# Own rows of a message step kept as three bfloat16 parts and spread by a one-hot matrix, in a sparse two-layer graph kernel

## The chip, the core and the metric

The kernel runs on one core of a Trainium2 chip. A core has a matrix engine (TensorE, in the profile PE, with its weight loads listed apart as PEld), a vector engine (VectorE, DVE), a scalar engine (ScalarE, ACT), a general engine (GpSimd, POOL) that here issues the gathers, and a queue for plain transfers (SyncE, SP). The metric is the device time of one execution in microseconds. Three timed runs of the kernel before gave 449.30, 445.47 and 449.06 us, so the median is 449.06 us. One more execution was recorded by the hardware profiler; it took 498.16 us, with a span of 496.4 us from its first to its last instruction.

## What is computed

Two graph layers over 2708 nodes with 128 features and a sparse 0/1 adjacency matrix. Layer 0 is attention with four heads over the neighbours of each node, gated, added to x and normalised. Layer 1, which the change is about, is a message layer; with everything that does not matter here left out, the reference is

```python
s = node_feats @ msg_w[:, :D].T
d = node_feats @ msg_w[:, D:].T
messages = gelu(s[:, None, :] + d[None, :, :] + msg_b)
aggregated = einsum('ijd,ij->id', messages, adj)
new_feats = concatenate([node_feats, aggregated], -1) @ upd_w.T + upd_b
h = gelu(new_feats) + node_feats
...
return (h - mu) / sqrt(var + LN_EPS) * ln_w + ln_b
```

followed by adding x and one more normalisation. So every edge (i, j) needs the row d[j] of its neighbour, the row s[i] + msg_b of its own node, and the sum of the two.

## The kernel before

The nodes are cut into 22 blocks of at most R = 126 rows, the blocks into nine groups: block 0 alone, six groups of three, one of two, and the last block alone. Each block's edges are listed in chunks of 128; there are 103 chunks. In layer 0 the adjacency rows of a block are loaded, its edges found and numbered, the neighbours' rows fetched by indirect transfers (POOL, L1116), and the attention sums made. `finish` closes a group: gate, normalisation, the new x in `xs`, its transpose in `xT`. Then `half(b, 1, ...)` makes d for each block of the group (PE L1274, ACT copy L1276 into the right half of `sd`) and sends it to the table `d_t` in DRAM. When all of `d_t` is written, layer 1 begins.

Layer 1 runs over 33 jobs of up to four chunks, the last group of blocks first and block 0 last; function `message` builds one:

- POOL fetches d of the neighbours, one indirect transfer for each chunk (L1318), into a buffer `g`, of which there are six.
- At a block's first job, `half(b, 0, ...)` makes s of the block in the left half of `sd` (PE L1274, ACT L1276). Row R of `sd` holds msg_b.
- `spreader` turns the one-hot staircase `E16` (bfloat16, row r is one from the first edge of row r on) into edge-to-row indicators: a bfloat16 matmul with the difference matrix `diff` (PE L1128) and an ACT copy into the float32 buffer `t32` (L1131).
- PE multiplies `t32` with s (L1335, float32, one product for each chunk), so that each edge gets its own row's s + msg_b in a bank of the pool `pq`.
- DVE adds g and that bank (L1339), ACT takes the gelu (L1342), and PE adds the messages up by rows with an indicator `s32` that DVE makes from the row numbers (L1327, PE L1353), into a bank of `pk`.

After a group's last job `update` follows: L1371 (ACT), L1375 and L1376 (PE), L1379 (ACT), L1385 (PE), then some thirty small DVE operations from L1388 on, and the output (SP, L1406).

Accumulator memory has eight banks: `pk` 2, `pm` 2, `pq` 3, `pr` 1. Every engine works through its instructions strictly in the order in which the program issues them. That order is worked out when the kernel is built, by the class `Board`: each operation is given a cost, the ones it comes after, a rank, and a lag, which is the time from its end to the moment when another engine can use it (`LAG`: 0.35 us for PE, 0.25 for DVE, 0.3 for ACT). The board simulates the engines with these figures and issues the operations in the order of their simulated starts. The true waits on the chip follow from the data, not from the board.

## Time and profile before

| | value |
|---|---|
| timed runs, median of three | 449.06 us |
| profiled execution, its own time | 498.16 us |
| its span | 496.4 us |
| mean granted TensorE clock in it | 0.748 |
| first gather of layer 1 (L1318) issued | 305.12 us |
| last gather of layer 1 done issuing | 468.25 us |
| gathers of layer 1 | 103, mean 957 ns |

Read the page like this: the busy shares of engines are averages over two layers with different limits, so each layer has to be read by itself. A "releaser" is what ended an engine's idle time; "remote" or "another core or an unknown queue" is put there when no recorded instruction or transfer fits. The profiled execution is 49.1 us longer than the median of the timed runs.

### The profile page before, as it was taken

How to read it: one execution, taken by the hardware profiler on the slowest of the kernel's cores; microseconds unless marked ns; L12 is line 12 of the kernel's file. 1: busy time of each engine (PE TensorE's matmuls, PEld its weight loads, DVE VectorE, ACT ScalarE, POOL GpSimd, SP SyncE). 2: the span in 40 equal slices, each digit the busy share in tenths (PEclk: the TensorE clock that was granted, in tenths of full speed). 3: DMA queues.
4: the chain of work that ended last, by engine and by line, in shares of the span. 5: the costliest groups of instructions: out<-in, count | busy, mean ns of one | idle time of the engine just before them, and what ended most of it. 6: DMA issues, size and time to landing. Idle time of an engine off the chain costs nothing.

```text
span 496.4 us, 5950 instructions
## 1 busy us (share of the span) xinstructions
PE 302.9 (61%) x1474; PEld 237.7 (48%) x1474; DVE 317.3 (64%) x1461; ACT 253.7 (51%) x587; POOL 224.2 (45%) x313
## 2 busy tenths in 40 slices
PE   3657786867785866649666356406484767274750
PEld 2334464745464645436556235405363656253650
DVE  4859787768676869848873775105457685463363
ACT  2366677647565858848766378205352233131310
POOL 7300467565533525262535103773664555566400
PEclk9769769688877878977695656555977797788765
DMA  7955949897899695851779988824421122122100
GB/s 180 237 139 191 282 111 262 226 267 239 291 245 245 190 234 128 258 156 33 217 241 231 251 239 264 200 54 131 114 53 44 43 60 51 34 61 65 33 15 11
DMA packets 31488, 78.51 MB, mean 158 GB/s; under 512 B 5776, under 2 KB 17131, under 8 KB 31439
## 3 DMA queue, kind: packets, MB, share of 16 engines
q1 hardware_dynamic: 21830, 55.06, 38.1%
q0 software_dynamic: 9520, 22.91, 18.8%
q8 instruction: 13, 0.21, 0.2%
q14 instruction: 30, 0.25, 0.2%
q10 hardware_dynamic: 95, 0.09, 0.1%
HBM read 72.38 MB, written 5.66 MB: 157 GB/s over the span
## 4 chain that ended last, share of the span: by engine, by line
PE 25%; DVE 23%; DMA 18%; issue 11%; another core or an unknown queue 8%; POOL 7%; ACT 6%; SPq 0%; DVEq 0%; POOLq 0%
DMA g<-kv_t,idx 12%; POOL g L1116 5%; PE pq L1335 4%; PE pk L1353 4%; ACT junk L993 2%; PE pk L954 2%; PE pm L866 2%; DMA kv_t<-kv 2%; DVE raw L959 2%; PE pm L1128 2%; PE pq L1087 2%; PE pr L1166 2%; POOL g L1318 2%; DMA sd<-in_x_dram 2%
## 5 line engine op out<-in xcount | busy, mean ns | idle before, releaser
L1116 POOL DMA_INDIRECT g<-kv_t,idx x103 | 99.8, 969 | 137.5 <-DMA abuf<-in_adj_dram 30.6
L1318 POOL DMA_INDIRECT g<-d_t,idx x103 | 98.5, 957 | 93.9 <-issue 55.2
L999 ACT ACTIVATE junk<-abuf,minus_one 126x1356 bf16<-126x1356 f32 (+15 forms) x44 | 62.8, 1427 | 7.9 <-DMA abuf<-in_adj_dram 7.9
L1131 ACT COPY t<-pm 127x384 f32<-127x384 f32 (+3 forms) x75 | 33.0, 453 | 66.1 <-remote 37.3
L1087 PE MATMUL pq<-rq,t 127*128 127x146 f32 (+3 forms) x206 | 49.8, 390 | 24.5 <-DVE qe L1147 14.5
L993 ACT ACTIVATE junk<-abuf 126x1356 bf16<-126x1356 uint32 (+15 forms) x44 | 58.8, 1335 | 0.2
L1335 PE MATMUL pq<-sd,t 127*128 127x128 f32 x206 | 37.7, 335 | 33.4 <-DVE kv L1339 15.2
L1087 PEld LDWEIGHTS pq<-rq,t 127*128 127x128 f32 x206 | 41.1, 255 | 32.2 <-DVE qe L1147 18.2
L1166 PE MATMUL pr<-val,s 128*126 128x136 f32 x206 | 47.2, 379 | 14.2 <-DVE val L1156 10.7
L1327 DVE TENSOR_TENSOR s<-iota,rid 128x504 f32<-128x504 f32 (+3 forms) x33 | 18.2, 565 | 58.0 <-remote 39.6
L1335 PEld LDWEIGHTS pq<-sd,t 127*128 127x128 f32 x206 | 34.8, 246 | 38.4 <-issue 29.4
L1166 PEld LDWEIGHTS pr<-val,s 128*126 128x126 f32 x206 | 39.9, 267 | 21.1 <-DVE val L1156 10.4
L954 PE MATMUL pk<-abuf,lkey 128*128 128x452 bf16 (+2 forms) x134 | 41.2, 411 | 11.8 <-DMA abuf<-in_adj_dram 4.2
L1353 PE MATMUL pk<-s,kv 128*128 128x126 f32 (+4 forms) x206 | 37.5, 334 | 5.5 <-ACT kv L1342 4.6
L1353 PEld LDWEIGHTS pk<-s,kv 128*128 128x128 f32 x206 | 34.0, 242 | 9.7 <-ACT kv L1342 7.4
L1147 DVE TENSOR_TENSOR qe<-pq,g 128x384 f32<-128x384 f32 (+2 forms) x42 | 20.1, 479 | 27.5 <-DMA g<-kv_t,idx 23.7
L1128 PE MATMUL pm<-E,diff 127*127 127x384 bf16 (+3 forms) x75 | 27.1, 377 | 16.0 <-ACT t L1131 4.4
L1274 PE MATMUL pm<-fwT,fxT 128*126 128x128 f32 x88 | 22.7, 365 | 14.8 <-issue 6.1
L959 DVE MAX8 raw<-pk 128x8 f32<-128x452 f32 (+39 forms) x59 | 24.9, 456 | 8.6 <-PE pk L954 3.8
L1274 PEld LDWEIGHTS pm<-fwT,fxT 128*126 128x126 f32 x88 | 18.8, 262 | 22.5 <-issue 10.1
L1342 ACT ACTIVATE kv<-kv 128x512 f32<-128x512 f32 (+3 forms) x33 | 17.3, 535 | 23.7 <-DVE kv L1339 15.8
L1339 DVE TENSOR_TENSOR kv<-g,pq 128x512 f32<-128x512 f32 (+3 forms) x33 | 18.3, 566 | 13.3 <-DMA g<-d_t,idx 12.7
(188 smaller groups left out, 628.0 us busy)
## 6 DMA issues: line engine op xcount, KB each, us to landing
abuf<-in_adj_dram SPq DMA_DIRECT2D x35, 667.4 KB
abuf<-in_adj_dram SPq DMA_DIRECT2D x35, 665.4 KB
kv_t<-kv SPq DMA_DIRECT2D x5, 528.0 KB
g<-kv_t,idx POOLq DMA_INDIRECT x103
g<-d_t,idx POOLq DMA_INDIRECT x103
xs<-in_x_dram POOLq DMA_DIRECT2D x22, 63.0 KB
sd<-in_x_dram SPq DMA_DIRECT2D x3, 448.0 KB
d_t<-sd SPq DMA_DIRECT2D x14, 63.0 KB
```

The lines of the kernel that those rows point to most:

```text
L954: nc.tensor.matmul(pt["at"][:, : c1 - c0], lkeys[k], low[:, 2 * c0 + 1 : 2 * c1 : 2], start=k == 0, stop=k == fold - 1)
L959: nc.vector.max(keyed["at"][:, k * CAP : (k + 1) * CAP], pt["at"][:, s0 - lo : s1 - lo])
L993: return board.add("ACT", 0.4 + 0.00085 * w, lambda: nc.scalar.activation(one.tile([P, FOLD * KW], BF16, name="junk")[:rows, :w], at.bitca ...
L999: return board.add("ACT", 0.4 + 0.00092 * w, lambda: nc.scalar.activation(one.tile([P, FOLD * KW], BF16, name="junk")[:rows, :w], at[:rows ...
L1087: nc.tensor.matmul(pq["at"][:, c * W : (c + 1) * W], t32["at"][:R1, c * P : (c + 1) * P], rq["at"][:R1, :W], start=True, stop=True)
L1116: nc.gpsimd.indirect_dma_start(out=g["at"][:, c * TW : (c + 1) * TW], out_offset=None, in_=kv_t[:, :], in_offset=bass.IndirectOffsetOnAxis ...
L1128: a = board.add("PE", pe(m * P, 1, False), lambda: nc.tensor.matmul(pt["at"][:R1, : m * P], diff[:R1, :R1], E16[:R1, o : o + m * P], start ...
L1166: nc.tensor.matmul(total["at"][:R, k * w : (k + 1) * w], s32["at"][:, c * R : (c + 1) * R], val["at"][:, c * w : (c + 1) * w], start=ch + ...
L1274: a = board.add("PE", pe(D), lambda: nc.tensor.matmul(pd["at"][:R, :D], xT[:, i : i + R], wT[:, h, :], start=True, stop=True), after=after ...
L1318: nc.gpsimd.indirect_dma_start(out=g["at"][:, c * D : (c + 1) * D], out_offset=None, in_=d_t[:, :], in_offset=bass.IndirectOffsetOnAxis(ap ...
L1335: nc.tensor.matmul(pz["at"][:, c * D : (c + 1) * D], t32["at"][:R1, c * P : (c + 1) * P], sd[:R1, b, :D], start=True, stop=True)
L1353: nc.tensor.matmul(agg["at"][:, o : o + n], mz["at"][:, c * D : (c + 1) * D], s32["at"][:, c * R : c * R + n], start=j == first_job[b] and ...
```

## The change

Own rows s are made for each group in layer 0, right after d, by a new function `near`. The steps from each row to the next (difference matrix times s, with msg_b folded in) are made in float32 and split into three bfloat16 parts whose sum is the float32 value. The parts of all blocks are kept. In layer 1 the staircase `E16` is multiplied with the three parts in one accumulation, so that a sum of steps gives the row; the matmul with `diff`, the copy into `t32` and the making of s are no longer there. `far` makes d for a whole group with one copy. The message banks are three of `pq` and two of `pm`, and the board is told that PE's hand-offs take 8.0 us in layer 1, but for the first four and last five jobs. Core of the diff:

```diff
-    sd = const.tile([P, NB, 2 * D], F32, name="sd")
+    sd = const.tile([P, NB, D], F32, name="sd")
+    own_s = [const.tile([P, GROUP, D], F32, name=f"own_s{i}") for i in range(2)]
...
+    difft = const.tile([P, P], F32, name="difft")
+    low_s = const.tile([P, NB, D], BF16, name="low_s")
+    high_s = sd.rearrange("p b d -> p (b d)").bitcast(BF16).rearrange("p (k b d) -> p k b d", k=2, d=D)
...
+        pu = psum("pm")
+        a = board.add("PE", 0.3, lambda: nc.tensor.transpose(pu["at"][:R1, :R1], below[:R1, :R1], ident[:R1, :R1]),
+                      after=[a_prep], make=[pu], rank=4, start=40.0)
+        stepped.append(board.add("ACT", act(P), lambda: nc.scalar.copy(difft[:R1, :R1], pu["at"][:R1, :R1]),
+                                 after=[a], use=[pu], rank=4))
...
-        for b in bs_:
-            half(b, 1, [a_x, weighted], rank)
...
+        x_in[gi] = a_x
+        far(gi, [a_x, weighted], rank)
+        near(gi, rank + 2.0)
+
+    def far(gi, after, rank):
...
+        def others():
+            for k, b in enumerate(g):
+                i = blocks[b][0]
+                nc.tensor.matmul(pd["at"][:R, k * D : (k + 1) * D], xT[:, i : i + R], wT[:, 1, :], start=True, stop=True)
+
+        a = board.add("PE", pe(D, len(g)), others, after=after, make=[pd], rank=rank)
+        a = board.add("ACT", act(w), lambda: nc.scalar.copy(dt["at"][:R, :w], pd["at"][:R, :w]), after=[a], use=[pd, dt],
+                      make=[dt], rank=rank)
...
+    def near(gi, rank):
...
+        ps, pd, r = psum("pm"), psum("pm"), temp("qe")
...
+        a = board.add("PE", pe(D, n), own, after=[x_in[gi], weighted, steps_of.get(gi - 2)], make=[ps], rank=rank)
+        a = board.add("ACT", act(w), lambda: nc.scalar.copy(
+            own_s[gi % 2][:R, :n, :], ps["at"][:R, :w].rearrange("p (k d) -> p k d", d=D)), after=[a], use=[ps], rank=rank)
+
+        def step():
+            for k, b in enumerate(g):
+                nc.tensor.matmul(pd["at"][:R1, k * D : (k + 1) * D], difft[:R1, :R1], own_s[gi % 2][:R1, k, :], start=True, stop=True)
+
+        steps_of[gi] = a = board.add("PE", pe(D, n), step, after=[a] + stepped, make=[pd], rank=rank)
+        a = board.add("ACT", act(w), lambda: nc.scalar.copy(part(0), pd["at"][:R1, :w]), after=[a], use=[pd], rank=rank)
+        a = board.add("DVE", dve(w), lambda: nc.vector.tensor_tensor(r["at"][:R1, :w], pd["at"][:R1, :w], part(0), ALU.subtract),
+                      after=[a], use=[pd, r], make=[r], rank=rank)
+        a = board.add("ACT", act(w), lambda: nc.scalar.copy(part(1), r["at"][:R1, :w]), after=[a], use=[r], rank=rank)
+        a = board.add("DVE", dve(w), lambda: nc.vector.tensor_tensor(part(2), r["at"][:R1, :w], part(1), ALU.subtract),
+                      after=[a], use=[r], rank=rank)
+        nears.append(a)
...
+    def slow(j):
+        return 8.0 if 4 <= j < len(jobs) - 5 else 0.35
...
-        g, t32, s32, mz = temp("g"), temp("t32"), temp("s32"), temp("kv")
+        g, s32, mz = temp("g"), temp("s32"), temp("kv" if j % 5 in (1, 3) else "t32")
...
-        if j == first_job[b]:
-            s_of[b] = half(b, 0, [sent[-1]], rank - 2.5)
-        a_t = spreader(ch, m, t32, sent[-1], rank - 1.5)
...
-        pz = psum("pq")
+        pz = psum("pm" if j % 5 in (1, 3) else "pq")
...
-                nc.tensor.matmul(pz["at"][:, c * D : (c + 1) * D], t32["at"][:R1, c * P : (c + 1) * P],
-                                 sd[:R1, b, :D], start=True, stop=True)
-
-        a = board.add("PE", pe(D, m), spread, after=[a_t, s_of[b]], make=[pz], use=[t32], rank=rank)
+                for part in (2, 1, 0):
+                    nc.tensor.matmul(pz["at"][:, c * D : (c + 1) * D], E16[:R1, (ch + c) * P : (ch + c + 1) * P],
+                                     (low_s[:R1] if part == 2 else high_s[:R1, part])[:, b, :], start=part == 2, stop=part == 0)
+
+        a = board.add("PE", pe(D, 3 * m, False), spread, after=nears + sent, make=[pz], rank=rank - 1.5, lag=slow(j))
...
-                                 make=[agg] if k == 0 and j == first_job[b] else [], rank=rank)
+                                 make=[agg] if k == 0 and j == first_job[b] else [], rank=rank, lag=slow(j))
         if b == groups[gi][-1] and j == last_job[b]:
-            update(gi, chain["agg"], rank)
+            update(gi, chain["agg"], rank, slow(j))
```

In `update` the two PE operations (the products with the update weights, and the transposes) are given the same lag. Row R of both `own_s` buffers is filled with msg_b by one transfer each from POOL at the start, where before one transfer filled row R of `sd`.

## The prediction

> **What bounds the kernel now.** I read the page's chain first, then the waits, then a stretch of the timeline, then the windows. On the page, the engines' row, then the chain by engine:
>
> ```profile
> PE 302.9 (61%) x1474; PEld 237.7 (48%) x1474; DVE 317.3 (64%) x1461; ACT 253.7 (51%) x587; POOL 224.2 (45%) x313
> ...
> PE 25%; DVE 23%; DMA 18%; issue 11%; another core or an unknown queue 8%; POOL 7%; ACT 6%; SPq 0%; DVEq 0%; POOLq 0%
> ```
>
> No engine is full, and no engine holds the chain: time goes in handing work on. But 8% (8.4% in the longer list, 41.7 us) is time that no recorded instruction explains. The waits by engine and line say where:
>
> ```profile
> DVE s L1327 <- remote: 39.6, 7, 17.1
> ACT t L1131 <- remote: 37.3, 7, 9.6
> ```
>
> (total us, times, longest). Both lines take over something from PE: L1131 copies what L1128 made, L1327 overwrites an indicator that L1353 has read. One such place in the timeline (start, duration, engine, what; idle time before it in brackets):
>
> ```profile
> 453.03 0.27 PE L1128 MATMUL pm<-E,diff 127*127 127x256 bf16 x1
> ...
> 456.19 0.95 POOL L1318 DMA_INDIRECT g<-d_t,idx  x1 [0.30 <-issue]
> 456.65 0.68 DVE L1327 TENSOR_TENSOR s<-iota,rid 128x504 f32<-128x504 f32 x1 [5.40 <-remote]
> ...
> 459.66 0.37 ACT L1131 COPY t<-pm 127x256 f32<-127x256 f32 x1 [7.85 <-remote]
> ...
> 460.86 0.95 POOL L1318 DMA_INDIRECT g<-d_t,idx  x1 [3.73 <-DVE kv L1339]
> ```
>
> PE is done at 453.30, ACT gets the result 6.4 us later. POOL has issued gathers back to back since 442.3. When POOL is quiet (399.10 to 399.57) the same hand-off takes 0.1 us. So in this execution PE's completions arrive late in long runs of gathers; at 322 to 339 us by up to 17 us. In the end the gather buffers aren't freed, and POOL itself waits.
>
> Is that so in the timed runs? They have 449.06 us, the profiled execution 498.16; the 49.1 us between are about the 41.7 us of unknown waits. Of these pieces 5.7 us lie in layer 0 and 35.8 in layer 1 (3.51, 2.51, 10.51, 3.76, 7.88, 5.38, 2.25). Without them layer 1 is 496.4 - 305.1 - 35.8 = 155 us. POOL's floor for it is 103 x (0.957 + 0.30 issue) = 129.5, plus the 28.1 us from the last gather to the end: 157.6. The two agree. I read it so: **the late hand-offs belong to the recording, and in the timed runs layer 1 is already bound by POOL's gathers.** Layer 0 is then some 294 us, bound by no one engine. Its windows (PE, PEld, DVE, ACT, POOL busy us and counts, granted clock, transfers' share, GB/s):
>
> ```profile
> 60.00:300.00 240.00, 163.65 (x805) 126.30 (x804) 176.00 (x826) 163.47 (x401) 105.96 (x119) 0.75 0.76 215
> ```
>
> PE 68%, DVE 73%, ACT 68%: three engines in fixed orders with little slack.
>
> **What the Trainium skill says.** "NOTIFIC — the notification-queue block", section 7.1, says that the unit that writes the trace's records holds its producers back rather than lose a record inside; with the stall this can put on an engine, a cause is there that untimed recording lacks. The trace has PE as the engine with most records and late completions, which fits, but doesn't prove it. "Perfetto Trace Analysis", summary of the profiler window per engine type, says that PE's recorded end is an estimate and semaphore propagation is hidden; so the lateness shows only as a wait with no releaser, as here. It also says that a gather's recorded end is the end of descriptor making; the trace agrees: the first three gathers end issuing at 308.6, their consumer starts at 315.04.
>
> **The change, part by part.** Group costs used:
>
> ```profile
> L1131 ACT COPY t<-pm 127x384 f32<-127x384 f32 (+3 forms) x75 | 33.0, 453 | 66.1 <-remote 37.3
> ...
> L1335 PE MATMUL pq<-sd,t 127*128 127x128 f32 x206 | 37.7, 335 | 33.4 <-DVE kv L1339 15.2
> ...
> L1128 PE MATMUL pm<-E,diff 127*127 127x384 bf16 (+3 forms) x75 | 27.1, 377 | 16.0 <-ACT t L1131 4.4
> L1274 PE MATMUL pm<-fwT,fxT 128*126 128x128 f32 x88 | 22.7, 365 | 14.8 <-issue 6.1
> ```
>
> *Added to layer 0, PE.* Own rows move from layer 1: 22 products, 44 instructions (each float32 product has two) at 22.7/88 = 0.258 us: 11.4. Steps are new: 22 products of the same shape, 11.4. Together 22.7 us; PE goes to 78% of these windows. The one transpose for `difft` is below 0.5.
> *ACT.* A group copy costs 0.481 (127x384), 0.374 (256) or 0.265 (128 wide, L1276): 6, 1 and 2 groups make 3.79 us. There are four sets (d, own, two parts), 15.2, and 22 copies of 0.265 = 5.8 go: +9.3.
> *DVE.* Two subtractions for each group at 0.558 (126x384, L1243), 0.42, 0.28: 2 x 4.33 = +8.7.
> *Queues.* SP has the same 22 sends of d; POOL one small transfer more at the start. Nothing.
> *On the path.* Nothing waits for the parts until layer 1, so what they cost is pushing others back. Priced by each engine's share of the chain: 22.7 x 25% + 8.7 x 23% + 9.3 x 6% = **+8.2 us**. New waits: `step` on PE waits for ACT's copy, which can stand behind a count of 1.43 us (L999), with the key products L954 and attention sums L1166 queued behind it, for which DVE waits; and `near` holds both banks of `pm`, which L1128 and L1099 need. Bounds: -5 (all in gaps, and a third of PE's 14.8 us of waits before L1274 goes, since d needs nine copies) to +23 (PE pays all).
>
> *The seam.* The last group's seven hops, about 4 us, lie beside the 9.9 us from the first gather to its use at 315.04: 0; without that cover +4.
>
> *Taken from layer 1.* PE: 33 of L1128 at 27.1/75 = 0.361: 11.9; own rows 11.4; float32 spreads 37.7. In their place 309 bfloat16 products. The nearest row, L1099 (127x126 bfloat16), has 13.6/103 = 0.132 each; the skill's "TensorE: Matmul & The Clock Gate", Back-to-back issue gap, has about 81 ns for 128 columns in a stream, which no run here shows. That is 25 to 41 us, estimate 32. Sum: PE -28. ACT: 33 x 0.44 + 22 x 0.25 = -20.
> DVE keeps all its work there (L1339, L1327, the updates), POOL its 129.5. So these 28 and 20 us are mostly off the path. POOL's 163.1 us window has 33.6 us of idle time; 25.1 follow the late hand-offs, 8.5 don't. With spreads five jobs ahead and no `t32` I give back half of the 8.5: **-4.2**, bounds -8.5 and 0.
>
> *The assumed 8.0 us.* They only set orders. The update of blocks 1 to 3 is put some 24 us behind its last message, so at the end of block 0's gathers. In the profiled execution its DVE work (469.9 to 479.0) stood before the last add at 479.8, though the last gather had been issued by 468.25. If the timed runs were that late, the new order gains up to 9; if DVE kept up there, the update was hidden under 18 gathers and is now put towards the end. I take **+2**, bounds -9 and +6.
>
> **Sum.** +8.2 - 4.2 + 2 = +6: 449 to **455 us** for the timed runs. Against the profiled execution's own 498.16 I expect less, 485 to 500, for there five banks cover part of the late hand-offs. Its time is not my forecast.
>
> **Rivals.** (1) *As forecast*, layer 0 pays more than layer 1 gives: 451 to 463; 45%. (2) *The late hand-offs are in the timed runs too.* For it: they recur in one place after another, and always in runs of gathers. Against: the 49 us between the profiled and the timed runs would need another cause. Five banks hold 5 x 3.1 x 1.257 = 19.5 us of gathers, more than the longest wait of 17.1; so 25.1 of POOL's idle and up to 9 at the end can go, against +8.2: 423 if all of it goes, 436 with half; around 432, 29%. It decides from about 13 us of recovered waits on. (3) *Layer 0 hides everything*: PE has 76 us of gaps in those 240. 449 - 4.2 + 2 = 447; 13%. (4) *PE pays all of it in layer 0*, 22.7, and the new order fails at the end, +4: 472 less what layer 1 gives, 468; 13%. That spreads don't do what they should is excluded by the algebra: sums of steps are rows.
>
> **The numbers.** 1% (4.5 us) is about what a measurement of this kernel can tell from no change. Faster: rival 2, 0.29. Same (444.6 to 453.5): rival 3 and a sixth of the first case, 0.21. Slower: 0.50. The range 433 to 467 leaves out half of rival 2 and half of rival 4, about 0.2. The likeliest case's own range is 451 to 463.
>
> **What would show it.** In the changed kernel's profile: the first L1318 some 8 us later than 305.1 if layer 0 pays; PE busy in its windows up by about 22 us; no L1131 or L1128 after it; 309 spreads at 80 to 130 ns; POOL in layer 1 near 1.257 us for each gather; "remote" waits left only on DVE. I am wrong if the first gather comes no later, or if the timed runs fall by more than the 8.5 us that POOL's other idle time allows; then the hand-offs were late without the recorder.

## The result, and the profile after

| | before | after |
|---|---|---|
| timed runs of the comparison, median | 447.64 us (445.47 to 449.30, 4 runs) | 475.36 us (471.38 to 476.59, 4 runs) |
| span of the profiled execution | 447.6 us (recorded in a quiet set, see below) | 469.6 us |
| first gather of layer 1 issued | 299.4 us | 312.4 us |
| last gather done issuing | 429.8 us | 443.8 us |
| from there to the end | 17.8 us | 25.8 us |

The ratio is 1.0607, with an interval of [1.0521, 1.0693]: slower by 27.7 us. Ratios are taken over the fast runs of each kernel and medians over all of its runs, so the two can differ by some us.

The kernel before takes about 448 us in some sets of runs and 496 to 499 us in others, so that everything below is compared inside its own set, and the recording of before that the prediction was read from (498.16 us) is of the second kind. Call the sets *quiet* and *late*, for what their recordings show: in the late ones the other engines wait for results of PE in layer 1, in the quiet ones they don't. The comparison above, and the profile of after, are quiet. So the profile in the column "before" is the unchanged kernel recorded once more in a quiet set; there the rows "DVE s L1327 <- remote" and "ACT t L1131 <- remote", which carried the prediction's first step, do not exist.

The changed kernel's line numbers move: the layer-1 gather L1318 is L1371, the spread L1335 is L1386, the indicator L1327 is L1377, the add L1339 is L1390, the gelu L1342 is L1393, the sums L1353 are L1404, the update's L1371, L1379, L1385, L1388 and L1403 are L1422, L1430, L1436, L1439 and L1454; in layer 0 the gather L1116 is L1129, the attention sums L1166 are L1179 and the count L993 is L1006.

The pages' rows of engines, of after and then of before in a quiet set (busy us, share of the span, instructions):

```profile
PE 291.4 (62%) x1589; PEld 228.2 (49%) x1589; DVE 325.0 (69%) x1480; ACT 242.3 (52%) x547; POOL 225.2 (48%) x314
```

```profile
PE 287.5 (64%) x1474; PEld 226.6 (51%) x1474; DVE 316.3 (71%) x1461; ACT 252.7 (56%) x587; POOL 224.6 (50%) x313
```

No engine got much busier (PE +3.9, DVE +8.7, ACT -10.4 us), and the kernel is 22 us longer. The loss is in order and waits. Nor is it the clock: up to the first gather of layer 1 the granted clock is 0.80 after and 0.79 before. POOL's groups on the two pages say that layer 1 itself did not move:

```profile
L1371 POOL DMA_INDIRECT g<-d_t,idx x103 | 100.3, 974 | 61.2 <-DMA d_t<-dt 30.1
```

```profile
L1318 POOL DMA_INDIRECT g<-d_t,idx x103 | 99.3, 964 | 65.7 <-DMA abuf<-in_adj_dram 34.6
```

103 gathers of 974 and 964 ns with 0.30 us between them: 131.4 us from first to last after, 130.4 before, and no pause above 0.6 us between them in either. The spans therefore differ by +13.0 (layer 0) +1.0 (gathers) +8.0 (end) = 22.0 us. The remaining 5.7 us to the timed difference are that after's profiled run is the quickest of its four (471.38), 4.0 below their median, and before's (449.37) is 1.7 above the 447.64.

**Layer 0.** Where its end is late is read from the chain of waits between the last gather of layer 0 (issued at 281.36 in after) and the first of layer 1 (start us, us, what):

```profile
296.80 0.49 ACT dt L1296
...
303.73 0.26 ACT dt L1296
...
304.76 0.66 PE pm L1324 x4
...
305.44 0.02 ACT sd L1327
...
305.70 1.43 ACT junk L1006 x2
307.13 0.15 ACT dt L1296
...
307.58 4.02 DMA d_t<-dt
...
312.42 1.14 POOL g L1371
```

L1296 is the copy of d that its transfer waits for, three times for the last three groups: 296.8, 303.7, 307.1. L1324 (`step`) and L1327 (copy of the first part) belong to `near`. They stand on the chain ahead of the last group's d, and a count of 1.4 us (L1006) is fitted between. All 22 blocks' d must be in memory before the first gather, so whatever of `near` stands before the *last* d delays layer 1, although nothing in layer 0 waits for its results. This is the smaller part, though: experiment 3 shows that most of the delay is there before this stretch begins.

**The end.** In the timeline of after (start, duration, engine, what; idle time before it in brackets), block 0's update and that of blocks 1 to 3:

```profile
448.17 0.84 PE L1436 MATMUL pm<-fident,qe 128*126 128x128 f32 x3
...
450.29 0.29 DVE L1439 TENSOR_TENSOR h<-pm,xs 126x128 f32<-126x128 f32 x1 [3.69 <-PE pm L1436]
455.57 0.35 DVE L1454 TENSOR_SCALAR h<-h,mv,rs 126x128 f32<-126x128 f32 x1
455.83 0.55 DVE L1439 TENSOR_TENSOR h<-pm,xs 126x384 f32<-126x384 f32 x1
463.28 0.86 DVE L1454 TENSOR_SCALAR h<-h,mv,rs 126x128 f32<-126x128 f32 x3
```

The same in the kernel before, quiet:

```profile
417.22 0.55 DVE L1388 TENSOR_TENSOR h<-pm,xs 126x384 f32<-126x384 f32 x1
427.14 0.86 DVE L1403 TENSOR_SCALAR h<-h,mv,rs 126x128 f32<-126x128 f32 x3
...
436.59 0.29 DVE L1388 TENSOR_TENSOR h<-pm,xs 126x128 f32<-126x128 f32 x1 [3.84 <-PE pm L1385]
441.85 0.35 DVE L1403 TENSOR_SCALAR h<-h,mv,rs 126x128 f32<-126x128 f32 x1
```

Before, the update of three blocks (the rows with 126x384 and x3) runs at 417 to 428, under gathers that go on to 429.8. After, it is last of all on DVE: from 455.83 to 464.14, 8.3 us behind block 0's, though PE had delivered its input by 449.0.

### The profile page after: what moved, and what is told of

Its sections match the earlier page's. It is cut to its first block, busy times and chain, and to the rows that moved or that the text cites. A ratio compares the mean times of both kernels' runs of the same rounds, so it can differ in the third digit from the quotient of the medians.

```text
span 469.6 us, 6156 instructions
## 1 busy us (share of the span) xinstructions
PE 291.4 (62%) x1589; PEld 228.2 (49%) x1589; DVE 325.0 (69%) x1480; ACT 242.3 (52%) x547; POOL 225.2 (48%) x314
## 5 line engine op out<-in xcount | busy, mean ns | idle before, releaser
L1129 POOL DMA_INDIRECT g<-kv_t,idx x103 | 98.6, 958 | 143.3 <-DVE idx L1125 29.6
L1371 POOL DMA_INDIRECT g<-d_t,idx x103 | 100.3, 974 | 61.2 <-DMA d_t<-dt 30.1
L1006 ACT ACTIVATE junk<-abuf 126x1356 bf16<-126x1356 uint32 (+15 forms) x44 | 58.8, 1336 | 0.3
L1179 PE MATMUL pr<-val,s 128*126 128x136 f32 x206 | 45.2, 366 | 16.1 <-DVE val L1169 13.9
L1160 DVE TENSOR_TENSOR qe<-pq,g 128x384 f32<-128x384 f32 (+2 forms) x42 | 20.1, 481 | 47.4 <-DMA g<-kv_t,idx 47.4
L967 PE MATMUL pk<-abuf,lkey 128*128 128x452 bf16 (+2 forms) x134 | 41.2, 412 | 14.4 <-DVE raw L972 4.7
L1179 PEld LDWEIGHTS pr<-val,s 128*126 128x126 f32 x206 | 38.5, 257 | 22.1 <-DVE val L1169 17.4
L1386 PEld LDWEIGHTS <-E 127*128 127x128 bf16 x309 | 27.7, 128 | 36.2 <-issue 19.8
L1393 ACT ACTIVATE t<-t 128x512 f32<-128x512 f32 (+3 forms) x20 | 11.1, 554 | 63.5 <-DVE t L1390 60.1
L1377 DVE TENSOR_TENSOR s<-iota,rid 128x504 f32<-128x504 f32 (+3 forms) x33 | 18.2, 564 | 24.0 <-PE pk L1404 24.0
L1386 PE MATMUL pq<-low_s,E 127*128 127x128 bf16 x66 | 16.7, 268 | 24.9 <-DVE t L1390 23.2
L1166 ACT ACTIVATE e<-score 128x12 f32<-128x12 f32 (+2 forms) x42 | 8.8, 211 | 43.0 <-DVE score L1163 42.7
L1404 PE MATMUL pk<-s,t 128*128 128x126 f32 (+4 forms) x132 | 26.2, 354 | 7.5 <-ACT t L1393 7.4
L1404 PEld LDWEIGHTS pk<-s,t 128*128 128x128 f32 x132 | 22.6, 254 | 9.6 <-ACT t L1393 9.6
L967 PEld LDWEIGHTS <-lkey 128*128 128x128 bf16 x134 | 14.2, 114 | 25.6 <-issue 8.6
L1393 ACT ACTIVATE kv<-kv 128x384 f32<-128x384 f32 (+3 forms) x13 | 6.6, 507 | 37.6 <-DVE kv L1390 37.6
L972 DVE MAX8 raw<-pk 128x8 f32<-128x452 f32 (+39 forms) x59 | 24.8, 457 | 1.4 <-PE pk L967 1.3
L1390 DVE TENSOR_TENSOR t<-g,pq 128x512 f32<-128x512 f32 (+3 forms) x20 | 11.8, 590 | 19.9 <-DMA g<-d_t,idx 19.9
L1169 DVE TENSOR_TENSOR val<-g,e 128x408 f32<-128x408 f32 (+2 forms) x42 | 20.6, 496 | 2.6 <-ACT e L1166 1.8
```

What stands on the lines that cost most here:

```text
L967: nc.tensor.matmul(pt["at"][:, : c1 - c0], lkeys[k], low[:, 2 * c0 + 1 : 2 * c1 : 2], start=k == 0, stop=k == fold - 1)
L972: nc.vector.max(keyed["at"][:, k * CAP : (k + 1) * CAP], pt["at"][:, s0 - lo : s1 - lo])
L1006: return board.add("ACT", 0.4 + 0.00085 * w, lambda: nc.scalar.activation(one.tile([P, FOLD * KW], BF16, name="junk")[:rows, :w], at.bitca ...
L1129: nc.gpsimd.indirect_dma_start(out=g["at"][:, c * TW : (c + 1) * TW], out_offset=None, in_=kv_t[:, :], in_offset=bass.IndirectOffsetOnAxis ...
L1179: nc.tensor.matmul(total["at"][:R, k * w : (k + 1) * w], s32["at"][:, c * R : (c + 1) * R], val["at"][:, c * w : (c + 1) * w], start=ch + ...
L1371: nc.gpsimd.indirect_dma_start(out=g["at"][:, c * D : (c + 1) * D], out_offset=None, in_=d_t[:, :], in_offset=bass.IndirectOffsetOnAxis(ap ...
```

## The experiments

Quiet sets: the four kernels of 1, the two of 3 and the one of 4. Late sets: those of 2 and 5, and the ones that are called late in 3 and 4. All durations of parts are from one recording each. How far such parts repeat is seen from orders that are the same in layer 0: kernels with after's layer 0 issue the first gather at 312.4, 315.1, 318.3 and 320.8; kernels with before's at 299.4 and 295.1. So a part is known to some 4 us, and sizes are better taken from medians of timed runs.

### 1. The kernel before again; the 8.0 us taken out; `near` taken out

The kernel before, unchanged:

> The kernel before, unchanged, recorded once more. If the late hand-offs of PE belong to the one recording of 498 us, this recording has a span near 447 us, hardly any wait without a releaser, first gather of layer 1 near 290 to 297 us, POOL's gathers of layer 1 back to back for about 131 us, and 18 to 22 us from the last gather to the end. If they are in every run, some 40 us of such waits come back and the first gather is near 260.

Measured: 449.54 us, 1.0032 [0.9996, 1.0069] to before in the same set; no wait put down to "remote" anywhere. The late hand-offs of the first recording don't belong to every recording.

The changed kernel with one number changed:

```diff
-        return 8.0 if 4 <= j < len(jobs) - 5 else 0.35
+        return 0.35
```

> The changed kernel with PE's assumed hand-off at 0.35 us for all jobs; layer 0 is as in the changed kernel. Theory order: the 8.0 us put the update of blocks 1 to 3 behind that of block 0, so the end gets shorter by about 8 us: 475 to 467. Theory layer 0 (all of the loss is the work added there): no difference, 473 to 477. Theory late hand-offs (the order with 8.0 us is what keeps POOL going): slower than 475, with pauses in the gathers.

Measured: 467.23 us, ratio 1.0391 [1.0243, 1.0539]; first gather at 318.3, last done at 449.9, 17.9 us to the end.

Only the last jobs relieved of it:

```diff
-        return 8.0 if 4 <= j < len(jobs) - 5 else 0.35
+        return 8.0 if 4 <= j < len(jobs) - 9 else 0.35
```

> The changed kernel with 8.0 us only up to the tenth job from the end instead of the sixth, so that only the last updates move forward. Theory order: the same gain as with 0.35 us everywhere, about 8 us (467). Theory layer 0: 473 to 477. If the gain of 0.35 us everywhere comes from the middle of layer 1, this one gains nothing.

Measured: 467.44 us, ratio 1.0439 [1.0252, 1.0626]; 18.5 us to the end. So the price of the assumed 8.0 us lies in the four jobs ahead of the last five. By the timeline they hold the update of blocks 1 to 3, which here ends on DVE at 450.8, ahead of block 0's at 458.5. Relieved, the end is as short as before's 17.8, and the median falls by 475.4 - 467.4 = 8.0 us; by the ratios it is 7.5 us here, 9.7 in the run above and 8.0 in its repetition under 3.

`near` left out, so that own rows are missing from the result; the spreads keep their number and shapes and multiply zeros:

```diff
+    nc.gpsimd.memset(low_s, 0.0)
...
-        near(gi, rank + 2.0)
...
-                                     (low_s[:R1] if part == 2 else high_s[:R1, part])[:, b, :], start=part == 2, stop=part == 0)
+                                     low_s[:R1, b, :], start=part == 2, stop=part == 0)
```

> The changed kernel without own rows, steps and their three parts (the spreads multiply zeros of the same shape instead; own rows are left out of the result). Theory layer 0: the first gather comes 10 to 18 us earlier than 312.4 and the time falls by as much, to 457 to 465. Theory order: the time falls by less than 4 us, for the added work lies in gaps. My forecast's own price was 8 us, which would give 467.

Measured: 462.02 us, ratio 1.0380 [1.0257, 1.0504]; first gather at 300.3, 12 us earlier than in after, 25.6 us to the end. The median falls by 13.3 us, the ratio by 10. The two losses are separate: this takes the first and leaves the second, the other two the reverse.

### 2. Which engine pays for `near`: inconclusive

Four kernels were timed in one set, which was a late one (before 496.09 us): `near` moved behind layer 0 (told under 3), no `near` with 0.35 us, and `near` cut to either half. Without `near`:

```diff
+    nc.gpsimd.memset(low_s, 0.0)
...
-        near(gi, rank + 2.0)
...
-        return 8.0 if 4 <= j < len(jobs) - 5 else 0.35
+        return 0.35
...
-                                     (low_s[:R1] if part == 2 else high_s[:R1, part])[:, b, :], start=part == 2, stop=part == 0)
+                                     low_s[:R1, b, :], start=part == 2, stop=part == 0)
```

> The changed kernel without near (own rows are left out of the result: the spreads multiply zeros, same count and shapes) and with 0.35 us everywhere. Theory of two separate costs: both are gone, so first gather about 300 us, end about 18 us, 449 to 452 us in all. Rival (the two costs share a cause, or the short order only moves waits about): 456 us or more.

Measured: 509.18 us, 1.0293 [1.0213, 1.0374], first gather at 316.6. For the same kernel in another late set this was expected:

> The changed kernel without near (own rows are left out of the result: the spreads multiply zeros) and with 0.35 us everywhere. On a chip where the kernel before takes about 448 us: first gather about 300 us, end about 18 us, 449 to 452 us if the two costs are separate; 456 us or more if they share a cause. On a chip where it takes about 496 us: ratio about 1.03, as measured there.

Measured: 509.62 us against 497.31, first gather at 309.0. The theory's 449 to 452 us was meant for a quiet set, so neither theory is decided.

PE's half of `near` (no second and third part):

```diff
...
-        a = board.add("DVE", dve(w), lambda: nc.vector.tensor_tensor(r["at"][:R1, :w], pd["at"][:R1, :w], part(0), ALU.subtract),
-                      after=[a], use=[pd, r], make=[r], rank=rank)
-        a = board.add("ACT", act(w), lambda: nc.scalar.copy(part(1), r["at"][:R1, :w]), after=[a], use=[r], rank=rank)
-        a = board.add("DVE", dve(w), lambda: nc.vector.tensor_tensor(part(2), r["at"][:R1, :w], part(1), ALU.subtract),
-                      after=[a], use=[r], rank=rank)
...
+                                     high_s[:R1, 0, b, :], start=part == 2, stop=part == 0)
```

> The changed kernel with near cut to PE's part of it: own rows, their copy, the steps and the first part's copy stay; the second and third parts (two DVE subtractions and one ACT copy for each group) are left out, and the spreads multiply the first part three times. First gather in the changed kernel at 312.4 us, without near at 300.3. Theory A (PE's 22.7 us of products and the hand-offs between PE and ACT cost): first gather at 309 us or later. Theory B (DVE, the busiest engine, pays for the subtractions): 303 us or earlier. Order and end are as in the changed kernel, so the whole is the first gather plus 158 us.

Measured: 503.33 us, 1.0172 [1.0090, 1.0254], first gather at 307.3.

The other half (no own rows, no steps; parts made from the product for d; the main lines of the edit):

```diff
...
-        a = board.add("PE", pe(D, n), own, after=[x_in[gi], weighted, steps_of.get(gi - 2)], make=[ps], rank=rank)
...
-        steps_of[gi] = a = board.add("PE", pe(D, n), step, after=[a] + stepped, make=[pd], rank=rank)
...
+        a = steps_of[gi]
...
+                                     low_s[:R1, b, :], start=part == 2, stop=part == 0)
```

> The changed kernel with near cut to its other half: no own rows and no steps (44 float32 products of PE and one ACT copy for each group are left out), but two ACT copies and two DVE subtractions for each group stay, made from the product for d, and the spreads multiply zeros. Theory A (PE pays): first gather at 303 us or earlier. Theory B (DVE pays): 309 us or later. If both this and the kernel with PE's part alone lie in the middle, the cost is shared.

Measured: 511.34 us, 1.0276 [1.0170, 1.0382], first gather at 311.1. The expectations were made for 300.3 without and 312.4 with all of `near`; in late sets the kernel without it had 309.0 and 316.6, so 307.3 and 311.1 decide nothing. In late sets even the whole of `near` can't be priced: the kernel without it took longer there (509.2 us) than the one that makes it behind layer 0 (504.5 us). Which engine pays is left open.

### 3. `near` behind layer 0

`near` is issued at each group's first message instead of in layer 0, and nothing is assumed late:

```diff
-        near(gi, rank + 2.0)
...
+        a = board.add("PE", pe(D, n), own, after=[x_in[gi], weighted, sent[-1], steps_of.get(gi + 2)], make=[ps], rank=rank)
...
-        return 8.0 if 4 <= j < len(jobs) - 5 else 0.35
+        return 0.35
...
+        if b == groups[gi][0] and j == first_job[b]:
+            near(gi, rank - 2.5)
...
+        a = board.add("PE", pe(D, 3 * m, False), spread, after=[nears_of[gi]] + sent, make=[pz], rank=rank - 1.5, lag=slow(j))
```

Set against the changed kernel with 0.35 us (experiment 1), which differs from it only in where `near` stands, in one quiet set:

> The changed kernel with 0.35 us instead of 8.0 us everywhere. On a chip where the kernel before takes about 496 us, the changed kernel had a ratio of 1.043 [1.034, 1.053], pauses of up to 8.4 us between gathers and 34 us to the end. Theory (the 8.0 us cannot help, since every engine stands still in the same stretches whatever the order): ratio 1.03 to 1.05 here too. Rival (the order fits late hand-offs and earns there what it loses elsewhere): ratio above 1.055. On a chip where the kernel before takes about 448 us: 467 us, as measured.

> The changed kernel with the own rows and steps made in layer 1 just ahead of each group's first message, and 0.35 us everywhere. On a chip where the kernel before takes about 448 us: theory (only near in layer 0 and the 8.0 us order cost) first gather at 299 to 302 us, 17 to 19 us to the end, 450 us in all; rival 455 us or more. On a chip where it takes about 496 us: ratio 1.01 to 1.03, and below the ratio of the kernel with near in layer 0 and the same 0.35 us.

Measured: 467.62 us with `near` in layer 0, ratio 1.0429 [1.0353, 1.0504]; 453.22 us with it behind, 1.0201 [1.0162, 1.0239]. The place of `near` alone is 14.4 us by the medians and 10 us by the ratios. First gather at 301.7, gathers 131.5 us, 18.1 us to the end. The expected 450 us was 3 too low and the rival's 455 not reached: 5.3 us over before remain by the medians, 9 by the ratio, of which the recordings show 2.3 in layer 0, 1.1 in the gathers and 0.3 at the end. No run separates what this rest is made of.

Where layer 0 loses is seen from its progress. Each group ends with the writing of its normalised rows (L1253 in before, L1266 in after). The last five groups began that at these times (us), and then came the first gather of layer 1:

| | 5th | 6th | 7th | 8th | 9th | first gather |
|---|---|---|---|---|---|---|
| before, quiet | 235.7 | 254.2 | 274.8 | 282.8 | 286.1 | 299.4 |
| after | 246.4 | 274.3 | 291.6 | 298.5 | 303.9 | 312.4 |
| `near` left out (experiment 1) | 241.8 | 258.1 | 275.7 | 284.6 | 290.7 | 300.3 |
| `near` behind layer 0 | 244.7 | 259.5 | 277.7 | 287.4 | 293.5 | 301.7 |

At the fifth group after and the last kernel are within 2 us of each other. At the sixth, after is 14.8 us behind, and later it loses no more. From the fifth to the sixth it takes 27.9 us, the other three 14.8 to 18.5. Shortly before the fifth group's end POOL, which fetches the rows for attention, stands for 12.1 us in after (12.1 to 13.0 in all four quiet recordings with `near` in layer 0). In the four quiet recordings without it no pause of POOL that ends between 220 and 260 us is above 5.9 us. The gathers behind that pause, first in after, then with `near` behind layer 0:

```profile
243.50 0.95 POOL L1129 DMA_INDIRECT g<-kv_t,idx  x1 [12.07 <-DVE eq L1122]
```

```profile
243.41 0.94 POOL L1129 DMA_INDIRECT g<-kv_t,idx  x1 [3.37 <-DVE rs_y L1210]
```

In after, the edge numbers that the gather needs (L1119 to L1125 on DVE) stand behind attention work (L1160) that itself waits for the rows of the gathers before, until 238.2. So POOL waits for the numbers and DVE for the rows. This reading of the timeline was not tested by a run. What the recordings show is that the long stretch goes with `near`: it is 27.2 to 29.5 us in all seven that have `near` or either half of it in layer 0, in quiet and late sets, and 14.8 to 20.4 us in the thirteen that don't. Either half brings it, so it looks like the issue order that the board finds with the added work, more than the work of one engine; that is not shown.

The end of layer 0 gives much less. Windows from the issue of the last gather of layer 0 to the first of layer 1 (from:to, length, then busy us and counts of PE, PEld, DVE, ACT, POOL, granted clock, transfers' share, GB/s), first after, then this kernel:

```profile
281.36:312.42 31.06, 17.18 (x81) 13.98 (x82) 24.56 (x102) 21.40 (x47) 0.94 (x2) 0.61 0.86 248
```

```profile
278.65:301.68 23.03, 11.15 (x41) 8.69 (x40) 17.62 (x73) 16.07 (x35) 0.95 (x2) 0.50 0.82 240
```

The 8.0 us between them can't be put down to `near`: the orders differ, and after has three jobs of attention left behind its last gather, this kernel one (18 sums L1179 against 7). Before, with no `near` at all and three such jobs, the stretch is 35.5 us. The fairer measure is from the start of the last normalised rows to the transfer of the last d. With `near` behind layer 0:

```profile
293.51 0.50 ACT xs L1266
...
296.15 0.17 ACT dt L1295
...
296.59 4.15 DMA d_t<-dt
...
301.68 0.94 POOL g L1370
```

That is 3.1 us, and 3.1 without `near`. With `near` in layer 0 it is 3.7 us in after and 4.2 in the other three quiet recordings. So the pieces of `near` that stand ahead of the last d cost about 1 us.

Three late sets of the same kernel, with what was expected there:

> The changed kernel, but each group's own rows and steps are made in layer 1, just ahead of its first message, and nothing is assumed late (0.35 us everywhere). Theory (near in layer 0 costs the 12 us, the 8.0 us order costs the 8 us at the end, nothing else matters): first gather at 299 to 302 us, last gather done about 131 us later, 17 to 19 us to the end, some 450 us in all, not told from the kernel before. Rival (the parts' copies and subtractions stand ahead of the adds on DVE and ACT and hold the gather buffers): gaps of POOL in layer 1, gathers taking 135 us or more, 455 us or more. Second rival (the 309 bfloat16 products are themselves slower at the end): end above 20 us.

> The changed kernel with the own rows and steps made in layer 1 just ahead of each group's first message, and 0.35 us everywhere. On a chip where the kernel before takes about 448 us: first gather at 299 to 302 us, some 131 us of gathers, 17 to 19 us to the end, 450 us in all (theory: only near in layer 0 and the 8.0 us order cost); 455 us or more if the parts' copies and subtractions hold up the adds. On a chip where the kernel before takes about 496 us: as measured there, ratio 1.01 to 1.03.

> The changed kernel with the own rows and steps made in layer 1 just ahead of each group's first message, and 0.35 us everywhere. On a chip where the kernel before takes about 448 us: theory (only near in layer 0 and the 8.0 us order cost) first gather at 299 to 302 us, some 131 us of gathers, 17 to 19 us to the end, 450 us in all; rival (the parts' copies and subtractions hold up the adds, or layer 0 is longer for another reason) 455 us or more. On a chip where the kernel before takes about 496 us: ratio 1.01 to 1.03, as before.

Measured: 504.51, 505.22 and 512.03 us, ratios 1.0174 [1.0083, 1.0265], 1.0144 [1.0051, 1.0237] and 1.0296 [1.0235, 1.0357]. It is faster than the changed kernel in both kinds of set, and slower than the kernel before in both.

### 4. The 8.0 us alone, in the kernel before

```diff
-                                 make=[agg] if k == 0 and j == first_job[b] else [], rank=rank)
+                                 make=[agg] if k == 0 and j == first_job[b] else [], rank=rank, lag=slow(j))
...
-        a = board.add("PE", pe(w, 2), dense, after=[a], make=[pu], use=[at], rank=rank)
+        a = board.add("PE", pe(w, 2), dense, after=[a], make=[pu], use=[at], rank=rank, lag=lag)
...
-        a = board.add("PE", pe(P, n) * 0.7, turn, after=[a], make=[pt], use=[tt], rank=rank)
+        a = board.add("PE", pe(P, n) * 0.7, turn, after=[a], make=[pt], use=[tt], rank=rank, lag=lag)
```

> The kernel before with 8.0 us instead of 0.35 assumed for the hand-offs of the sums by rows and of the updates' two products, and nothing else. In a set where the kernel before takes about 448 us: theory (the assumed 8.0 us alone puts the update of blocks 1 to 3 last) the end grows from 17.8 to 24 to 27 us, the first gather stays at 299 to 301 us, 454 to 457 us in all; rival (the longer end needs the bfloat16 spreads) end 18 us, 448 us. In a set where it takes about 496 us: ratio 0.99 to 1.01, as before.

(`slow` is that of the changed kernel.) Measured in the quiet set: 453.91 us against 449.62, ratio 1.0142 [1.0036, 1.0247]. That is 4.3 us by the medians and 6.4 by the ratio, at the lower edge of the theory's 454 to 457. The end is 24.8 us instead of 17.8, as expected; the first gather came at 295.1, some 4 us before the expected time. The timeline shows the same picture as in after, with lines moved by four (L1392 is L1388, L1407 is L1403):

```profile
437.30 0.55 DVE L1392 TENSOR_TENSOR h<-pm,xs 126x384 f32<-126x384 f32 x1
439.44 0.35 DVE L1407 TENSOR_SCALAR h<-h,mv,rs 126x128 f32<-126x128 f32 x1
445.03 0.86 DVE L1407 TENSOR_SCALAR h<-h,mv,rs 126x128 f32<-126x128 f32 x3
```

The three-block update (126x384, x3) ends last. So the assumption alone brings the longer end, without bfloat16 spreads or kept parts. The same kernel in two late sets:

> The kernel before with one edit alone: 8.0 us instead of 0.35 assumed for the hand-offs of the sums by rows and of the updates' two products (the spreads keep 0.35). On a chip where the kernel before takes about 448 us: theory (the assumed 8.0 us puts the update of blocks 1 to 3 behind everything) the end grows from 17.8 to 24 to 27 us, the first gather stays at 299 to 300, 454 to 457 us. Rival (the longer end belongs to the bfloat16 spreads or the three parts): end 18 us, 448 us. On a chip where it takes about 496 us: theory, the same 5 to 9 us more; rival (there the longer assumption fits the facts): less time than the kernel before.

> The kernel before with 8.0 us instead of 0.35 assumed for the hand-offs of the sums by rows and of the updates' two products, and nothing else. On a chip where the kernel before takes about 448 us: theory (the assumed 8.0 us puts the update of blocks 1 to 3 last) the end grows from 17.8 to 24 to 27 us, 454 to 457 us; rival (the longer end needs the bfloat16 spreads) end 18 us, 448 us. On a chip where it takes about 496 us: ratio 0.99 to 1.00, as before.

Measured: 496.38 and 502.49 us, ratios 0.9948 [0.9899, 0.9996] and 1.0073 [1.0046, 1.0100]. Where hand-offs are late, the order earns or costs less than 1%, and not with the same sign twice.

### 5. The late sets

The changed kernel there:

> The changed kernel as it is, to be set against the kernel before on the same chip. The kernel before took 448 us on one chip and 496 us on another, where PE's results reached the others late in runs of gathers. If this chip is of the first kind: 470 to 476 us, ratio 1.05 to 1.07. If of the second kind, theory A (five banks and the assumed 8.0 us cover part of the lateness, as the order was made for): at most the time of the kernel before. Theory B (the cover is worth less than layer 0 and the end lose): ratio above 1.01, pauses of 8 us between gathers in spite of five banks.

Measured: 519.98 us, ratio 1.0434 [1.0341, 1.0526], 34.1 us to the end. Theory B holds. Its waits by engine and line (total us, times, longest), and one place in its timeline:

```profile
DVE s L1377 <- remote: 62.8, 11, 19.6
ACT qe L1430 <- remote: 18.1, 1, 18.1
```

```profile
350.06 0.95 POOL L1371 DMA_INDIRECT g<-d_t,idx  x1 [0.30 <-issue]
355.56 0.37 ACT L1430 ACTIVATE qe<-pr,upd_col 128x126 f32<-128x126 f32 x1 [18.15 <-remote]
355.64 0.55 DVE L1377 TENSOR_TENSOR s<-iota,rid 128x378 f32<-128x378 f32 x1 [19.63 <-remote]
...
359.36 0.95 POOL L1371 DMA_INDIRECT g<-d_t,idx  x1 [8.36 <-DVE badh L1473]
```

DVE stands 19.6 us at L1377 and ACT 18.2 us at L1430, both for something of PE, while POOL issues gathers until 351.0; then POOL stands for 8.4 us as well, and goes on at 359.36, just after an add (L1390, at 358.54) has freed a buffer. Five banks did not help: the adds that would free the buffers are queued on DVE *behind* L1377, which waits for PE's sums and needs no bank. The add of 358.54 takes over a bank that PE had filled by 336.7.

A theory was that PE's results get through only when POOL's run of gathers ends. To try it on the kernel before, POOL was to run at most three jobs ahead:

```diff
-        got = [board.add("POOL", 1.25, lambda c=c: fetch(c), after=sent, use=[g], make=[g] if c == 0 else [],
+        got = [board.add("POOL", 1.25, lambda c=c: fetch(c), after=sent + [added.get(j - 3)], use=[g], make=[g] if c == 0 else [],
...
-        a = board.add("DVE", dve(m * D), lambda: nc.vector.tensor_tensor(
+        added[j] = a = board.add("DVE", dve(m * D), lambda: nc.vector.tensor_tensor(
```

> The kernel before with one wait added: POOL fetches for a job only when the add of three jobs earlier is done, so that at most three jobs of gathers, about 12 us, can be issued without a result of PE. The orders of PE and DVE are the same as in the kernel before. Theory (on the chips where hand-offs are late, PE's results get through only when POOL's run of gathers ends): there the waits put down to remote get shorter, none above 12 us where the longest was 17, while pauses of 4 us or more between gathers come more often; in all not faster, 495 to 510 us. Rival (lateness has nothing to do with POOL's run): the longest stays at 15 to 17 us. On a chip where the kernel before takes about 448 us: adds are never three jobs behind, no change, 446 to 450 us.

Measured: 498.74 us, ratio 0.9983 [0.9949, 1.0016], and in its waits:

```profile
DVE s L1327 <- remote: 36.3, 5, 17.8
ACT t L1131 <- remote: 26.6, 4, 9.6
```

The longest is 17.8 us where none above 12 was expected, but this does not refute the theory, because POOL was not held back. What `after` names is used by the board alone, to find an order; a wait on the chip arises only from data, and no data goes from an add to POOL. The gathers around the longest wait show it:

```profile
304.15 0.94 POOL L1318 DMA_INDIRECT g<-d_t,idx  x1 [29.79 <-issue]
...
332.86 0.94 POOL L1318 DMA_INDIRECT g<-d_t,idx  x1 [0.30 <-issue]
339.50 0.94 POOL L1318 DMA_INDIRECT g<-d_t,idx  x1 [5.70 <-DVE h L1388]
```

From 304.15 to 333.8 POOL issues 24 gathers without a pause, eight jobs of three, though only two adds are done (313.69 and 316.94): two buffers come free and all six are filled again. The wait meant here would have stopped it after five jobs. The kernel before has a run of 24 at the same place. So this run is in effect the kernel before once more, and its ratio says so.

The theory stays untested. Three long waits ended alike after the last gather of a run was issued: 4.4 us after it here (333.8 and 338.2) and in the kernel before (334.8 and 339.2), 4.6 us in the changed kernel (351.0 and 355.6). Shorter ones end inside a run (ACT at 325.77 and 328.57 in the kernel before), and POOL stops because no buffer is free, so which comes first is not shown. A lower granted clock is not enough: the quiet recording of after has 0.764 and no such wait, a late one of experiment 4 has 0.779 and has them. What makes the hand-offs late in some sets stays open.

## Why the prediction went wrong, step by step

It said 455 us and came to 475.4; the direction was the likeliest one given, the size lies outside the range. In the quiet sets the loss divides, by medians, into 8.0 us (the assumed 8.0 us, experiment 1), 14.4 (`near` in layer 0, experiment 3) and a rest of 5.3; by ratios into 8, 10 and 9. The rest is what is left over, so the agreement of the sum proves nothing. Two terms of the prediction's sum failed, the assumed 8.0 us and what is added to layer 0. Against the steps:

- **"The assumed 8.0 us": +2, bounds -9 and +6.** It failed, outside its own bound: 8.0 (7.5 to 9.7 by the ratios; 4.3 to 6.4 in the kernel before). The text had the cost in its hand ("now put towards the end"), but it mixed it with a gain that only late hand-offs could give, and it bounded the loss at 6. The three-block update on DVE takes 8.3 us once it stands alone behind block 0's; that is the price. The prediction had the 9.1 us of the same update in its own recording (469.9 to 479.0).
- **"Added to layer 0": +8.2, bounds -5 to +23.** Mis-sized: 10 to 14 for the place of `near`, and 5 to 9 for a rest that no run separates and the sum had no term for. The amounts of work were not too low: own rows and steps together are 16.5 us of PE, not 22.7. The rows of after (busy us, mean ns):

```profile
L1316 PE MATMUL pm<-fwT,fxT 128*126 128x128 f32 x44 | 8.4, 333 | 2.0 <-ACT dt L1296 1.7 <-ACT t L1144 0.3
L1324 PE MATMUL pm<-own_s,difft 127*127 127x128 f32 x44 | 8.1, 320 | 2.8 <-ACT own_s L1319 2.6 <-ACT t L1144 0.2
```

  What failed is the pricing by shares of the chain. The cost did not come as added busy time spread over the layer, but in one stretch between the fifth and the sixth group, 27.9 us instead of 14.8, with a wait of 12.1 us at POOL's gathers. The step named new waits behind `near` and gave them no price of their own.
- **"The seam": 0, without cover +4.** It held within about 1 us: from the start of the last normalised rows to the transfer of the last d 3.7 us in after, 3.1 in before.
- **"Taken from layer 1": -4.2 for gather pauses, bounds -8.5 and 0.** There was nothing to take. In quiet runs of the kernel before no gather waits, so the 8.5 us of "other" pauses were part of the late recording too, and the gathers take 1.0 us more after. (PE's part there adds up to -29, not -28; nothing rests on it.)
- **"The late hand-offs belong to the recording."** Wrong as put: whole sets of timed runs take 496 to 499 us, and every recording made in those sets has such waits. For the runs it was meant for, the consequence holds: layer 1 is bound by POOL, 103 gathers in 130.4 us against the estimated 129.5. The reading of the Trainium skill's "NOTIFIC — the notification-queue block", section 7.1, as a cause has no support here: none of the eight recordings of quiet sets has such a wait. The end, taken as 28.1, was lengthened as well; it is 17.8.
- **Rival 2** (gain where hand-offs are late) fails on its own ground: 1.0434 in a late set. Its sum counted banks of accumulators, and DVE's wait at L1377 needs none. **Rival 4** had both mechanisms that came, PE paying in layer 0 and the order failing at the end, with 22.7 and +4. Its 468 leaves out the +4; its own terms add up to 472, which is nearest of all. Its 22.7 was PE's busy time, though, which is not what was paid.
- **What would show it:** "first L1318 some 8 us later" was 13.0; "PE busy up by about 22" was 9.6 (206.5 against 196.9 us up to the first gather); no L1131 or L1128 after it, right; gathers near 1.257 us, right; "remote" waits left only on DVE, in after there are none. "Profiled time 485 to 500" was 471.4, since that recording fell into a quiet set.

## What to carry to other kernels

Work that nobody waits for is not free: it is planned together with everything else, and the order found around it can hold a pause that the work itself does not explain. Before moving work into a stage, ask what it will stand ahead of on each engine; afterwards compare the progress of the stage part by part, for two windows at its end need not hold the same work. A pessimistic hand-off in a planner is not a margin of safety; it moves real work, and at the end of a kernel it moves it past the cover. A wait that only the planner knows is no wait on the chip: whether an engine was held back must be seen in the recording. If a profiled execution is 10% longer than the timed runs, its waits are those of another state, and the kernel should be read from a recording whose own time agrees.

## Not expected of the hardware

The same kernel took 448 us in some sets of runs and 496 to 499 us in others (443 to 454 us in one, 490 to 500 in another). In the second kind the recordings have waits for results of PE of up to 19.6 us in layer 1, with longer pauses of POOL behind them. Chip number 6 stood in a set of either kind.

The 309 bfloat16 spreads, of 80 to 130 ns expected, ran on the chain of after in groups of nine in 0.68 to 1.14 us, which is 75 to 127 ns each, and they freed nothing that the kernel was waiting for.
